# Node tiles 125 columns wide, laid side by side, in the mixer's operands and the turned layer norm of a graph layer on one Trainium2 core

## The chip, the cores and the metric

The kernel runs on one core of one Trainium2 chip. The metric is the device time of one execution in microseconds (us); lower is better. The time before is the median of three runs. The profile is of one further execution.

## The reference, cut to what matters

One GPS layer over a graph of 3125 nodes with 256 features: a normalised input, a graph convolution over 53125 edges, a linear-attention mixer over all nodes, and a mixture of 16 experts of which each node takes two.

```python
xn = layernorm(x)                                     # 3125 x 256
# graph convolution
agg = segment_sum(edge_weight[:, None] * xn[src], dst)
gnn = agg @ W.T + b
# linear attention, 8 heads of 32
Q, K = elu(xn @ Wq) + 1, elu(xn @ Wk) + 1
KV = sum over nodes of K (x) (xn @ Wv)                # per head
Z = 1 / (Q . sum(K) + eps)
msg = layernorm((Q KV Z) @ Wm) * g1 + b1
h = relu(concat([xn, msg]) @ W1) @ W2
mix = xn + layernorm(h) * g2 + b2
x = x + gnn + mix
# experts, on the normalised result
x = x + sum over the two best experts e of share_e * ((silu(y @ w1[e]) * (y @ w2[e])) @ w3[e])
```

## The kernel before

**Tiles.** The 3125 nodes are 25 tiles (`NT`) of 125 nodes (`V = 125`). A tile lies on the chip as 125 rows, one node to a partition, with three rows of padding up to `P = 128`. Where nodes run along columns (transposed operands), a tile has 128 columns, of which the last three belong to padding. All matrix products of 32-bit floats appear in the trace as two matmul records and two weight-load records each, products of 16-bit floats as one of each.

**Stage 1, node by node (to about 110 us).** For each tile, `normed` (line 409) makes the normalised rows `xn` and turns them with two transposes (line 428) into columns, which ScalarE copies into `xnT` (line 429), a buffer of 2 x 3200 columns. `projected` (line 431) uses the tile's 128 columns of `xnT` as the stationary operand (`lhsT`) against the weights `wcat` (lines 437 and 439), which gives the graph convolution's rows `y` (the product with W comes before the sum over edges), K and V; `y` stays in SBUF (`y_early`, `y_late`) and is also stored to `y_d` in DRAM by SyncE (line 449). `summed` (line 458) adds up K and V over the nodes; it already takes 125 rows. From tile 18 on, two adjacency blocks are built beside each tile.

**Adjacency (lines 328 to 360).** The edges become dense blocks: VectorE compares (`one`, line 335) and multiplies (`wone`, line 340), TensorE forms three products of 16-bit floats per block (line 355), ScalarE copies (line 358) and SyncE stores to `adj_d` in DRAM. All operands there have 128 columns.

**Stage 2, the mixer (about 110 to 550 us).** Seven groups of 4, 4, 4, 4, 3, 3 and 3 tiles. For a group of `nt` tiles the columns lie side by side, `w = nt * P` wide (512 or 384). `asked` (line 468) makes the queries: products with moving operand `xnT[..., c0 : c0 + w]` (line 477), the denominators with moving operand `qT` (line 489), a reciprocal and a product on VectorE in two parts (lines 494 and 495). `mixer` (line 631) takes for each tile a product with stationary `qT` (line 641), moments (`stats`, bn_stats and bn_aggr, lines 103 and 104), `rsqrt` (a chain of small VectorE instructions, lines 91 to 98), the norm (line 649), two transposes (line 653) and a copy into `mT` (line 654). This is the turned layer norm. Then the hidden layer with moving operands `xnT` and `mT`, `w` columns wide (line 662), its activation (line 664), and per tile a product with stationary `hT` (line 673). Pieces of `asked` for the next group, adjacency blocks and messages are traced between the pieces of the mixer. `messages` (line 613) multiplies dense adjacency rows, read back from `adj_d` as `nbr`, with `y` (line 625: stationary `rows`, 128 x 128; moving `y_of(k)`, 128 x 256), and adds the result to `x_all` on VectorE (line 627).

**Stage 3 (about 550 to 705 us).** `last_messages` (line 731) does the last part of the messages (line 738), beside the gate and the routing. **Stage 4** are the experts (lines 955 to 1077), which the change doesn't touch.

**What sets the order.** The build lays the instructions of each engine in an order of its own: what is ready sooner comes sooner, so the order in the trace isn't the order of the text (five transposes of line 309 stand between two halves of line 437's products). `tc.issue_after(ins)` puts what a block issues behind `ins` on its engine; it is used at the points where the order is fixed by hand. The rings of buffers set the rest: `tok` three PSUM buffers, `big` two, `pa` two, `pb` one, `nbr` three.

Of the kernel before, what the change touches and what calls it, by code (L numbers as in the profile page):

```python
# [8 lines left out]
F32 = mybir.dt.float32  # L9
# [53 lines left out]
def tile_gps_layer(ctx: ExitStack, tc: tile.TileContext, a: dict, out: bass.AP):  # L63
# [4 lines left out]
    dram = ctx.enter_context(tc.tile_pool(name="dram", bufs=1, space=DRAM))  # L68

    xn_d = dram.tile([N, XW], F32, name="xn_d")  # L70
    y_d = dram.tile([NT * P, C], F32, name="y_d")
    first_d = dram.tile([NG, 1], I32, name="first_d")


# [8 lines left out]

    def rsqrt(var, n, with_last=False):

        v = small.tile([P, 13], F32, name="rs_v")[:, :n]
        hv = small.tile([P, 13], F32, name="rs_h")[:, :n]
        bits = small.tile([P, 13], I32, name="rs_b")[:, :n]
        y = small.tile([P, 13], F32, name="rs_y")[:, :n]
        s = small.tile([P, 13], F32, name="rs_s")[:, :n]  # L90
        nc.vector.tensor_scalar(v, var, LN_EPS, None, op0=ALU.add)
        nc.vector.tensor_scalar(hv, v, -0.5, None, op0=ALU.mult)
        nc.vector.tensor_scalar(bits, v.bitcast(I32), 1, None, op0=ALU.logical_shift_right)
        nc.vector.tensor_scalar(y.bitcast(I32), bits, -1.0, float(0x5F3759DF), op0=ALU.mult, op1=ALU.add)
        for _ in range(3):
            nc.vector.tensor_tensor(s, y, y, op=ALU.mult)
            nc.vector.tensor_tensor(s, s, hv, op=ALU.mult)
            found = nc.vector.scalar_tensor_tensor(y, s, 1.5, y, op0=ALU.add, op1=ALU.mult)
        return (y, found) if with_last else y

    def stats(mv, src):
        st = small.tile([P, 6], F32, name="bn_st")
        nc.vector.bn_stats(st, src)
        return nc.vector.bn_aggr(mv, st)

# [88 lines left out]
    later.append((gate_w, a["gate_w"].rearrange("(k p) e -> p k e", p=128)))  # L194
    cb = w_mix.tile([P, C], F32, name="cb")

    xnT = w_mix.tile([128, 2, NT * P], F32, name="xnT")

    Y0 = PARTS[-1][0]
    y_early = w_mix.tile([P, Y0, C], F32, name="y_early")  # L200
# [2 lines left out]
    def y_of(t):  # L203
        return y_early[:, t, :] if t < Y0 else y_late[:, t - Y0, :]
# [204 lines left out]
    def normed(t):  # L409

        nonlocal rstd, r0
        for t0, t1 in BATCHES:
            if t == t0:
                rstd, r0 = ready.pop(t0), t0
        xn = work.tile([P, C], F32, name="xn", bufs=4)
        ins = nc.vector.tensor_scalar(xn, x_all[:, t, :], mv[:, t, 0:1], rstd[:, t - r0 : t - r0 + 1],
                                      op0=ALU.subtract, op1=ALU.mult)
        with tc.issue_after(ins.ins):
            for batch in BATCHES:
                if t == batch[0]:  # L420
                    factors(*batch, rstd)
            for _ in range(LISTS.get(t, 0)):
                next(pieces, None)
            if t in AHEAD:
                moments(*AHEAD[t])
        ptr = a_ps.tile([128, 2, P], F32, name="tok", bufs=3)
        for k in range(2):
            nc.tensor.transpose(ptr[:, k, :], xn[:, k * 128 : (k + 1) * 128], ident)
        nc.scalar.copy(xnT[:, :, t * P : (t + 1) * P], ptr)

    def projected(t):

        cols = slice(t * P, (t + 1) * P)
        pyk = a_ps.tile([P, 2 * C], F32, name="big")
        pv = a_ps.tile([P, C], F32, name="tok", bufs=3)
        for k in range(2):
            nc.tensor.matmul(pyk, lhsT=xnT[:, k, cols], rhs=wcat[:, k, : 2 * C], start=(k == 0), stop=(k == 1))  # L437
        for k in range(2):
            last = nc.tensor.matmul(pv, lhsT=xnT[:, k, cols], rhs=wcat[:, k, 2 * C :], start=(k == 0), stop=(k == 1))
        ek = work.tile([P, C], F32, name="ek", bufs=2)  # L440
        nc.scalar.activation(ek, pyk[:, C:], AF.Exp)
        k_sb = work.tile([P, C], F32, name="k_sb")
        nc.scalar.activation(k_sb, pyk[:, C:], AF.Relu)

        nc.vector.scalar_tensor_tensor(k_sb, ek, 1.0, k_sb, op0=ALU.min, op1=ALU.add)
        v_sb = v_ring[t % 3]
        v_copy = nc.scalar.activation(v_sb[:, :, :128], pv.rearrange("p (c v) -> p c v", c=2), AF.Copy, scale=1.0 / N)
        nc.scalar.copy(y_of(t), pyk[:, :C])
        stored = nc.sync.dma_start(y_d[t * P : (t + 1) * P, :], y_of(t))
        with tc.issue_after(stored.ins):  # L450
            load_later(t)

        with tc.issue_after(v_copy.ins):
            nc.scalar.activation(x_all[:, t, :], x_all[:, t, :], AF.Identity, scale=by[:, t : t + 1],
                                 bias=less[:, t : t + 1])
        return last, k_sb, v_sb
# [10 lines left out]

    def asked(t0, nt):

        w = nt * P  # L470
        c0 = t0 * P
        qT = mix.tile([128, 2, GROUP * P], F32, name="qT")
        asked_for.append(qT)
        for c in range(2):
# [12 lines left out]
        for c in range(2):  # L487
            p = a_ps.tile([128, 512], F32, name="big")
            nc.tensor.matmul(p[:, :w], lhsT=ksum[:, c, :], rhs=qT[:, c, :w], start=True, stop=True)  # L489
            pz.append((p, mix.tile([128, GROUP * P], F32, name="eq")))  # L490
        for part in (slice(0, 2 * P), slice(2 * P, w)):
            for c, (p, z) in enumerate(pz):
                nc.scalar.activation(z[:, part], p[:, part], AF.Copy, bias=ATT_EPS / N, scale=1.0 / N)
                nc.vector.reciprocal(z[:, part], z[:, part])
                nc.vector.tensor_tensor(qT[:, c, part], qT[:, c, part], z[:, part], op=ALU.mult)
            yield
# [62 lines left out]
    with tc.If(n_loops > 0):  # L559
        with tc.For_i(0, n_loops, 1) as it:  # L560
# [17 lines left out]
            nc.vector.tensor_scalar(took, took, -1.0, 1.0, op0=ALU.mult, op1=ALU.add)  # L578
            nc.vector.tensor_tensor(took, took, r.bitcast(F32)[:, 2:3], op=ALU.mult)
            t_d, _, p_d = placed(dst_f, sel, [V, 1], "ld")  # L580
            nc.vector.scalar_tensor_tensor(t_d, t_d, float(P), p_d, op0=ALU.mult, op1=ALU.add)
            row_d = sel.tile([V, 1], I32, name="l_row")
            nc.vector.tensor_copy(row_d, t_d)
            g = sel.tile([V, C], F32, name="l_g")
# [28 lines left out]
    def messages(part, t, n, alone=False):  # L613

        t0, t1 = PARTS[part]

        if alone:
            pb = bank_a(2 * C)[:P].rearrange("p (a b) c -> p a (b c)", a=2)
        else:
            pb = b_ps.tile([P, 2, C], F32, name="pb")  # L620
        for i in range(n):
            rows = neighbours(part, t + i)
            for k in range(t0, t1):

                nc.tensor.matmul(pb[:, i, :], lhsT=rows[:, k - t0, :], rhs=y_of(k),  # L625
                                 start=(k == t0 and i == 0), stop=(k == t1 - 1), skip_group_check=True)
        nc.vector.tensor_tensor(x_all[:, t : t + n, :], x_all[:, t : t + n, :], pb[:, :n, :], op=ALU.add)  # L627

    early = [(part, t, min(2, NT - t)) for part in range(len(PARTS) - 1) for t in range(0, NT, 2)]

    def mixer(t0, nt, qT, following):

        w = nt * P
        c0 = t0 * P
        mv = small.tile([P, GROUP, 2], F32, name="mv_m")
        mw = mix.tile([P, GROUP, C], F32, name="mw")
        for i in range(nt):
            cols = slice(i * P, (i + 1) * P)
            pw = a_ps.tile([P, C], F32, name="tok", bufs=3)
            for k in range(2):  # L640
                nc.tensor.matmul(pw, lhsT=qT[:, k, cols], rhs=kvw[:, k, :], start=(k == 0), stop=(k == 1))
            stats(mv[:, i, :], pw)
            nc.scalar.copy(mw[:, i, :], pw)
            yield
# [3 lines left out]
        for i in range(nt):  # L648
# [1 line left out]
                                    op0=ALU.subtract, op1=ALU.mult)  # L650
            ptr = a_ps.tile([128, 2, P], F32, name="tok", bufs=3)
            for k in range(2):
                nc.tensor.transpose(ptr[:, k, :], mw[:, i, k * 128 : (k + 1) * 128], ident)
            nc.scalar.copy(mT[:, :, i * P : (i + 1) * P], ptr)
            yield

        hT = mix.tile([128, 4, GROUP * P], F32, name="hT", bufs=1)
        for j in range(4):
# [6 lines left out]
            yield  # L665
            if next(following, "end") != "end":
                yield
        mv2 = small.tile([P, GROUP, 2], F32, name="mv_m2")
        hw = mix.tile([P, GROUP, C], F32, name="mw")
        for i in range(nt):  # L670
            po = a_ps.tile([P, C], F32, name="tok", bufs=3)
            for j in range(4):
                nc.tensor.matmul(po, lhsT=hT[:, j, i * P : (i + 1) * P], rhs=w2[:, j, :],  # L673
                                 start=(j == 0), stop=(j == 3))
            stats(mv2[:, i, :], po)
            nc.vector.scalar_tensor_tensor(hw[:, i, :], po, mv2[:, i, 0:1], g2, op0=ALU.subtract, op1=ALU.mult)
            if i < nt - 1:
                yield
        rstd = rsqrt(mv2[:, :nt, 1], nt)
        for i in range(nt):  # L680
            xt = x_all[:, t0 + i, :]
            nc.vector.scalar_tensor_tensor(xt, hw[:, i, :], rstd[:, i : i + 1], xt, op0=ALU.mult, op1=ALU.add)

    t = 0
# [38 lines left out]
    def bank_out():  # L723
        return bank("po", 3)
# [6 lines left out]
    def last_messages(t):  # L731
# [1 line left out]
        t0, t1 = PARTS[part]  # L733

        rows = neighbours(part, t, nbr_2 if t % 5 in (3, 4) else nbr)
        pg = bank_out()[:, 0, :]
        for k in range(t0, t1):
            last = nc.tensor.matmul(pg, lhsT=rows[:, k - t0, :], rhs=y_of(k), start=(k == t0),  # L738
                                    stop=(k == t1 - 1))
        nc.vector.tensor_tensor(x_all[:, t, :], x_all[:, t, :], pg, op=ALU.add)  # L740
        stats(mv_g[:, t, :], x_all[:, t, :])
        nc.sync.dma_start(out[t * V : (t + 1) * V, :], x_all[:V, t, :])
        return last
# [548 lines left out]
```

## Time and profile before

| | us |
|---|---|
| median of three runs (1036.63 to 1038.35) | 1038.11 |
| the profiled execution | 1038.03 |
| its span, from the first instruction to the last | 1036.2 |
| TensorE matmul busy, 6006 records | 1007.1 |
| TensorE weight loads busy, 6006 records | 809.3 |
| VectorE busy, 1750 instructions | 655.3 |
| ScalarE busy, 577 instructions | 263.9 |
| GpSimd busy, 200 instructions | 216.1 |

Busy time of an engine is the union of its instructions' times. Matmul records overlap: one of 256 columns is listed with some 382 ns, while the next begins some 216 ns behind it. So the step from one record to the next is read from runs of equal records (in the chain or the timeline), not from a record's own duration. A line such as L625 is a line of the kernel; in a group's line `out<-in` names the tiles, then come the shapes (rows x columns of the array, then partitions x elements), the count, the busy time, the mean of one in ns and the idle time before them.

### The profile page before, as it was taken

To read this page: it belongs to the slowest core of one execution; us is meant where nothing else is said; L and a number is where in the kernel's file an instruction comes from. 1 tells how busy PE (TensorE), PEld (TensorE's weight loads), DVE (VectorE), ACT (ScalarE), POOL (GpSimd) and SP (SyncE) were. 2 spreads that over 40 slices of the span, in tenths; PEclk is the share of its full clock that TensorE was granted. 3 is DMA by queue.
4 is the path that set the end of the run, shared out by engine and by line. 5 is a ranking of instruction groups with operands and counts; after the bars stand their busy time and mean duration, and the time that the engine had idled before them with its cause. 6 is when DMAs were issued, how large, how long until landed. Compare 5 with 4: busy or idle time off the path is not lost.

```text
span 1036.2 us, 16279 instructions
## 1 busy us (share of the span) xinstructions
PE 1007.1 (97%) x6006; PEld 809.3 (78%) x6006; DVE 655.3 (63%) x1750; ACT 263.9 (25%) x577; POOL 216.1 (21%) x200
## 2 busy tenths in 40 slices
PE   7999999999999999999999999999999999999995
PEld 5667666686786887887877888887888888888884
DVE  8968699889787897956598148786932222222221
ACT  3666424323323233222141000103111111111110
POOL 3420100023100000000000001014445444545442
PEclk9999999999999999999999999999999999999998
DMA  6444104343344344553354455565757757667662
GB/s 214 95 131 145 53 31 167 128 140 136 122 137 138 133 162 133 175 181 143 140 182 155 159 167 166 183 194 179 209 155 226 240 170 234 199 202 225 206 189 26
DMA packets 70374, 165.09 MB, mean 159 GB/s; under 512 B 11091, under 2 KB 29934, under 8 KB 66314
## 3 DMA queue, kind: packets, MB, share of 16 engines
q1 hardware_dynamic: 53816, 138.10, 38.9%
q0 software_dynamic: 15520, 25.04, 10.7%
q8 instruction: 50, 0.82, 0.3%
q10 hardware_dynamic: 946, 0.79, 0.2%
q14 instruction: 42, 0.34, 0.1%
HBM read 105.85 MB, written 58.00 MB: 158 GB/s over the span
## 4 chain that ended last, share of the span: by engine, by line
PE 71%; DVE 10%; issue 1%; POOL 0%; ACT 0%; POOLq 0%; DVEq 0%; ACTq 0%
PE ph L1001 18%; PE pb L625 13%; PE po L1027 10%; PE po L738 8%; PE pa L355 6%; PE big L662 6%; PE tok L673 3%; DVE wone L340 2%; PE ptr L987 1%; PE pa L625 1%; PE big L477 1%; DVE one L335 1%; PE ph L799 1%; DVE wone L350 1%; PE big L489 1%
## 5 line engine op out<-in xcount | busy, mean ns | idle before, releaser
L1001 PE MATMUL ph<-xTb,wt 128*128 128x256 f32 (+2 forms) x992 | 204.5, 355 | 0.8 <-issue 0.8
L1001 PEld LDWEIGHTS ph<-xTb,wt 128*128 128x128 f32 x992 | 171.5, 190 | 24.9 <-ACT xTb L990 4.5
L625 PE MATMUL pb<-y_early,nbr 128*128 128x256 f32 x736 | 170.7, 382 | 0.4 <-DVE x_all L627 0.4
L340 DVE TENSOR_TENSOR wone<-one,wgts 128x1536 bf16<-128x1536 bf16 x150 | 140.6, 949 | 27.0 <-PE pa L355 26.8
L625 PEld LDWEIGHTS pb<-y_early,nbr 128*128 128x128 f32 x736 | 135.4, 190 | 17.2 <-DVE x_all L627 1.0
L355 PEld LDWEIGHTS <-one 128*128 128x128 bf16 x1875 | 117.3, 97 | 39.1 <-issue 19.1
L358 ACT COPY adj<-pa 128x512 f32<-128x512 f32 (+1 forms) x157 | 91.8, 586 | 194.2 <-PE pa L355 156.4
L355 PE MATMUL pa<-wone,one 128*128 128x128 bf16 x1875 | 130.3, 218 | 2.3 <-DVE wone L340 0.9
L1008 DVE TENSOR_TENSOR hid<-hid,ph 128x512 f32<-128x512 f32 (+2 forms) x62 | 38.3, 618 | 145.7 <-PE ph L1001 135.4
L1027 PE MATMUL po<-wt,hid 128*128 128x256 f32 (+1 forms) x456 | 115.2, 385 | 0.8 <-DVE yb L1030 0.7
L738 PE MATMUL po<-y_late,nbr 128*128 128x256 f32 x450 | 102.3, 381 | 0.5 <-DVE x_all L627 0.5
L335 DVE TENSOR_TENSOR one<-iota,keys 128x1024 bf16<-128x1024 bf16 x150 | 100.8, 692 | 0.7 <-POOL wgts L317 0.7
L1031 POOL DMA_INDIRECT out<-yb,to_l x45 | 70.9, 1576 | 114.4 <-DVE yb L1030 63.4
L1027 PEld LDWEIGHTS po<-wt,hid 128*128 128x128 f32 (+1 forms) x456 | 79.1, 184 | 17.6 <-DVE yb L1030 5.5
L738 PEld LDWEIGHTS po<-y_late,nbr 128*128 128x128 f32 x450 | 83.4, 190 | 11.2 <-DVE x_all L627 0.9
L1007 ACT ACTIVATE hid<-ph 128x512 f32<-128x512 f32 (+2 forms) x62 | 33.6, 542 | 208.4 <-PE ph L1001 204.4
L1030 DVE TENSOR_SCALAR yb<-po,sh 128x256 f32<-128x256 f32 (+1 forms) x57 | 27.5, 482 | 57.3 <-PE po L1027 54.9
L751 POOL IOTA rev<- 125x16 f32 x1 | 0.2, 156 | 296.5 <-PE pb L625 296.5
L700 POOL TENSOR_TENSOR x_all<-x_all,cb 128x256 f32<-128x256 f32 x25 | 25.7, 1050 | 148.2 <-DVE x_all L627 140.5
L627 DVE TENSOR_TENSOR x_all<-x_all,pb 128x512 f32<-128x512 f32 (+1 forms) x37 | 24.3, 655 | 41.8 <-PE pb L625 41.8
L662 PE MATMUL big<-xnT,w 128*128 128x512 f32 (+1 forms) x112 | 49.8, 556 | 0.0
L437 PE MATMUL big<-wcat,xnT 128*128 128x512 f32 x100 | 49.0, 612 | 0.0
(285 smaller groups left out, 1202.5 us busy)
## 6 DMA issues: line engine op xcount, KB each, us to landing
wt<-in_w SPq DMA_DIRECT2D x28, 1536.0 KB
adj_d<-adj SPq DMA_DIRECT2D x156, 256.0 KB
nbr<-adj_d SPq DMA_DIRECT2D x25, 576.0 KB
nbr<-adj_d SPq DMA_DIRECT2D x50, 256.0 KB
nbr<-adj_d SPq DMA_DIRECT2D x25, 512.0 KB
wt<-in_w POOLq DMA_DIRECT2D x3, 1536.0 KB
out<-x_all SPq DMA_DIRECT2D x25, 125.0 KB
x_all<-in_x SPq DMA_DIRECT2D x4, 640.0 KB
```

The lines of the kernel that those rows point to most:

```text
L335: nc.vector.tensor_tensor(one.rearrange("p b h e j -> p (b h) e j"), iota_2[:, None, :, :].to_broadcast(shape), ql.rearrange("p b h j -> p ...
L340: nc.vector.tensor_tensor(wone, one[:, :, 1:2, :, :].to_broadcast(shape), w[:, :, :, None, :].to_broadcast(shape), op=ALU.mult)
L355: nc.tensor.matmul(pa[:, j, :], lhsT=one[:, j // 2, 0, :, j % 2], rhs=wone[:, j // 2, i, :, j % 2], start=(i == 0), stop=(i == 2))
L358: copied = nc.scalar.copy(rows[:, :n, :], pa[:, :n, :])
L437: nc.tensor.matmul(pyk, lhsT=xnT[:, k, cols], rhs=wcat[:, k, : 2 * C], start=(k == 0), stop=(k == 1))
L625: nc.tensor.matmul(pb[:, i, :], lhsT=rows[:, k - t0, :], rhs=y_of(k), start=(k == t0 and i == 0), stop=(k == t1 - 1), skip_group_check=True)
L662: nc.tensor.matmul(ph[:, :w], lhsT=w1[:, k, j * 128 : (j + 1) * 128], rhs=rhs, start=(k == 0), stop=(k == 3))
L738: last = nc.tensor.matmul(pg, lhsT=rows[:, k - t0, :], rhs=y_of(k), start=(k == t0), stop=(k == t1 - 1))
L1001: last = nc.tensor.matmul(p[:, m, :w], lhsT=self.wt[:, i, k * F + at : k * F + at + 128], rhs=self.xT[:, k, :w], start=(k == 0), stop=(k = ...
L1008: self.units = nc.vector.tensor_tensor(hid, hid, pre[1], op=ALU.mult)
L1027: last = nc.tensor.matmul(po[:n_r, r, :], lhsT=self.hid[:, k, r * LANES : r * LANES + n_r], rhs=self.wt[:, 2, k * C : (k + 1) * C], start= ...
L1031: made.append(nc.gpsimd.indirect_dma_start(out=out[:, :], out_offset=bass.IndirectOffsetOnAxis(ap=at, axis=0), in_=yb[:n_r, r, :], in_offs ...
```

## The change

Wherever nodes run along columns in the mixer's operands, a tile now takes 125 columns, not 128: in `xnT` (2 x 3125 columns), in `qT`, `mT` and `hT`, so that a group is 500 or 375 columns wide, not 512 or 384. The transposes that make these columns read 125 rows (lines 428 and 653). What has these columns as its stationary operand then has 125 rows of output, and moments, norms and copies on them take 125 partitions. The messages take 125 rows and 125 columns of the adjacency block and 125 rows of `y`; the adjacency itself is built, stored and loaded as blocks of 128 as before. `y_d` has 3125 rows, and its store takes 125 rows. No instruction is added or removed.

```diff
-    y_d = dram.tile([NT * P, C], F32, name="y_d")
+    y_d = dram.tile([N, C], F32, name="y_d")
...
     def rsqrt(var, n, with_last=False):
-        v = small.tile([P, 13], F32, name="rs_v")[:, :n]
+        p = var.shape[0]
+        v = small.tile([P, 13], F32, name="rs_v")[:p, :n]
...
-    xnT = w_mix.tile([128, 2, NT * P], F32, name="xnT")
+    xnT = w_mix.tile([128, 2, N], F32, name="xnT")
...
-            nc.tensor.transpose(ptr[:, k, :], xn[:, k * 128 : (k + 1) * 128], ident)
-        nc.scalar.copy(xnT[:, :, t * P : (t + 1) * P], ptr)
+            nc.tensor.transpose(ptr[:, k, :V], xn[:V, k * 128 : (k + 1) * 128], ident[:V, :V])
+        nc.scalar.copy(xnT[:, :, t * V : (t + 1) * V], ptr[:, :, :V])
...
     def projected(t):
-        cols = slice(t * P, (t + 1) * P)
-        pyk = a_ps.tile([P, 2 * C], F32, name="big")
+        cols = slice(t * V, (t + 1) * V)
+        pyk = a_ps.tile([P, 2 * C], F32, name="big")[:V]
...
-        stored = nc.sync.dma_start(y_d[t * P : (t + 1) * P, :], y_of(t))
+        stored = nc.sync.dma_start(y_d[t * V : (t + 1) * V, :], y_of(t)[:V])
...
     def asked(t0, nt):
-        w = nt * P
-        c0 = t0 * P
+        w = nt * V
+        c0 = t0 * V
...
-        for part in (slice(0, 2 * P), slice(2 * P, w)):
+        for part in (slice(0, 2 * V), slice(2 * V, w)):
...
-                nc.tensor.matmul(pb[:, i, :], lhsT=rows[:, k - t0, :], rhs=y_of(k),
+                nc.tensor.matmul(pb[:V, i, :], lhsT=rows[:V, k - t0, :V], rhs=y_of(k)[:V],
...
     def mixer(t0, nt, qT, following):
-        w = nt * P
-        c0 = t0 * P
-        mv = small.tile([P, GROUP, 2], F32, name="mv_m")
-        mw = mix.tile([P, GROUP, C], F32, name="mw")
+        w = nt * V
+        c0 = t0 * V
+        mv = small.tile([P, GROUP, 2], F32, name="mv_m")[:V]
+        mw = mix.tile([P, GROUP, C], F32, name="mw")[:V]
         for i in range(nt):
-            cols = slice(i * P, (i + 1) * P)
-            pw = a_ps.tile([P, C], F32, name="tok", bufs=3)
+            cols = slice(i * V, (i + 1) * V)
+            pw = a_ps.tile([P, C], F32, name="tok", bufs=3)[:V]
...
-                nc.tensor.transpose(ptr[:, k, :], mw[:, i, k * 128 : (k + 1) * 128], ident)
-            nc.scalar.copy(mT[:, :, i * P : (i + 1) * P], ptr)
+                nc.tensor.transpose(ptr[:, k, :V], mw[:, i, k * 128 : (k + 1) * 128], ident[:V, :V])
+            nc.scalar.copy(mT[:, :, i * V : (i + 1) * V], ptr[:, :, :V])
...
-                nc.tensor.matmul(po, lhsT=hT[:, j, i * P : (i + 1) * P], rhs=w2[:, j, :],
+                nc.tensor.matmul(po, lhsT=hT[:, j, i * V : (i + 1) * V], rhs=w2[:, j, :],
...
     def last_messages(t):
-        pg = bank_out()[:, 0, :]
+        pg = bank_out()[:V, 0, :]
...
-            last = nc.tensor.matmul(pg, lhsT=rows[:, k - t0, :], rhs=y_of(k), start=(k == t0),
+            last = nc.tensor.matmul(pg, lhsT=rows[:V, k - t0, :V], rhs=y_of(k)[:V], start=(k == t0),
```

The same cut (`[:V]`) is made on the rows of `ek`, `k_sb`, `v_sb`, `y_of(t)`, `x_all`, `pv`, `po`, `hw` and `g2` where these lines use them.

## The prediction

> **What bounds the kernel now.** I read the busy shares first, then the chain that ended last, then the waits, then the groups by shape and single stretches of the timeline. The page's shares, and its chain by engine:
>
> ```profile
> PE 1007.1 (97%) x6006; PEld 809.3 (78%) x6006; DVE 655.3 (63%) x1750; ACT 263.9 (25%) x577; POOL 216.1 (21%) x200
> ...
> PE 71%; DVE 10%; issue 1%; POOL 0%; ACT 0%; POOLq 0%; DVEq 0%; ACTq 0%
> ```
>
> TensorE (PE) works for 97% of the span, and 71% of the chain is PE (this view loses the chain before 171 us, so its shares add up to 82%). A busy share alone proves little for PE, since its records overlap. So the waits of PE between 100 and 560 us, where the mixer runs:
>
> ```profile
> PE tok L653 <- DVE mw L649: 4.2, 5, 1.3
> PE tok L641 <- DVEq L559: 1.0, 1, 1.0
> PE big L489 <- ACT eq L493: 0.8, 1, 0.8
> ...
> PE pa L355 <- DVE wone L340: 0.4, 1, 0.4
> ```
>
> Columns: total us, times, longest. With four further waits of 0.4 to 0.6 us they make 8.3 us in 460. The one that repeats is the turned norm: PE's transposes (L653) wait for VectorE's norm (L649). Everywhere else PE's own rate is the time, so what counts is how long each matmul record holds PE. Three pieces of the chain give that, as start, length, what:
>
> ```profile
> 198.87 3.43 PE big L662 x8
> ...
> 400.53 2.63 PE big L662 x8
> ...
> 432.17 6.96 PE pb L625 x32
> ```
>
> Eight records of 512 moving columns took 3.43 us, 429 ns each; eight of 384 columns 2.63 us, 329 ns each; 32 of 256 columns 6.96 us, 217.5 ns each. (429 - 217.5) / 256 = 0.83 ns for each moving column of a 32-bit record, with only some 5 ns besides. The weight load (190 ns listed, overlapped) doesn't show in it.
>
> **What the change saves on PE.** Only moving operands along which nodes run get shorter; these are the groups:
>
> ```profile
> L662 PE MATMUL big<-xnT,w 128*128 128x512 f32 x64 | 31.2, 599 | 0.0
> L662 PE MATMUL big<-mT,w 128*128 128x512 f32 x64 | 30.5, 597 | 0.5 <-ACT mT L654 0.5
> ...
> L662 PE MATMUL big<-xnT,w 128*128 128x384 f32 x48 | 18.6, 500 | 0.0
> ```
>
> L662: 128 records go from 512 to 500 columns and 96 (48 from xnT, 48 from mT) from 384 to 375: 128 x 12 + 96 x 9 = 2400 columns. L477 (the groups list 32 and 24 records): 600. L489 (16 and 12): 300. The transposes L428 and L653, 50 records each, go from 128 to 125 columns: 300. Together 3600 columns x 0.83 ns = **3.0 us**. Line 437, 439, 641, 673, 625 and 738 have 125 stationary columns instead, and still 256 or 512 moving ones; at 0.83 ns per moving column they hold PE as long as before. I take 0 for them.
>
> That zero is the largest claim here, since these lines are 100 + 100 + 100 + 200 + 800 + 450 = 1750 records that get a stationary operand of 125 columns; the 1250 of L625 and L738 among them, and the 100 transposes, get 125 rows as well. The timeline of before has such shapes already (start, length, what):
>
> ```profile
> 61.30 0.61 PE L461 MATMUL pkv<-v_sb,k_sb 125*128 125x129 f32 x4
> 61.75 0.70 PE L309 MATMUL pa<-ident,key 125*128 125x125 f32 x5
> 62.28 0.38 PE L428 MATMUL tok<-ident,xn 128*128 128x128 f32 x2
> ```
>
> L461 takes 125 rows: the next record begins 0.45 us (61.75 - 61.30) after four of them, 113 ns each; L309, 125 rows and 125 moving columns, 0.53 us for five, 106 ns each; L428, 128 rows and columns, 110 ns each (62.28 to 62.50 for two). So 125 rows cost nothing over 128. Half of L461's moving operands start at byte 516 of their buffer (the second half of 2 x 129 columns), and the four still take 0.45 us: a start off a round boundary, as `xnT[..., t * 125]` now has, costs nothing either. For 125 stationary columns the weight loads say:
>
> ```profile
> L625 PEld LDWEIGHTS pb<-y_early,nbr 128*128 128x128 f32 x736 | 135.4, 190 | 17.2 <-DVE x_all L627 1.0
> L355 PEld LDWEIGHTS <-one 128*128 128x128 bf16 x1875 | 117.3, 97 | 39.1 <-issue 19.1 <-DVE wone L340 5.8 <-DVE wone L350 1.5
> ...
> L852 PEld LDWEIGHTS <-ones_h 125*125 125x125 bf16 x3 | 0.4, 138 | 0.2
> ...
> L243 PEld LDWEIGHTS pa<-heads,ones 125*125 125x125 f32 x2 | 0.3, 189 | 0.0
> ```
>
> A 16-bit load takes 97 ns with 128 columns and 138 ns with 125: 41 ns dearer for less work. A 32-bit load takes 190 ns with 128 and 189 ns with 125 (two records only). All loads that this change narrows are of 32-bit floats; the 16-bit ones (the adjacency, L355) keep 128. The Trainium skill, "TensorE: Matmul & The Clock Gate", section "Weight-path perf modes — Fast Weight Load (FWL) and DoubleRow", says that the fast load is on when the number of weights is 128 and the type isn't FP32; by that rule no narrowed load here was ever fast, and the sum is unchanged; the pair 97 / 138 agrees with it, and 190 / 189 too. Bounds for these 1750 loads: none below -3 ns each (three columns of a load; L1027's 64-column loads list 136 ns against 190, so 0.84 ns a column), hidden under 216 ns of matmul; above, 41 ns each, which is a rival below.
>
> **What else moves.** VectorE: the reciprocals L494 take 1726 ns for 256 columns and 936 for 128, 6.2 ns a column; 150 columns fewer over the seven groups, 0.9 us; L495 and L483 some 0.4 us. ScalarE: the copies and activations on these columns (L429, L654, L480, L481, L493, L664) lose 1050 columns at 0.85 ns, 0.9 us. These lie beside PE, so I count them at nothing; where they stand right before a wait of PE (L493 before L489, one wait of 0.8 us) they help by some 10 ns. Instructions on 125 instead of 128 partitions with the same number of elements per partition cost the same (L627, L649, L676 and the moments). SyncE: the stores to y_d (L449) take 125 rows; their issue lists 320 ns with 128 rows, and the stores of 125 rows to `out` (L742) list 289, and nobody waits for either. The loads of `nbr` and the stores of `adj_d` stay at 128. No wait is added and no step is moved in the text.
>
> **How much of the 3.0 us arrives at the end.** Before 171 us, PE runs nearly back to back. Behind it the chain holds 5.6% x 1036.2 = 58 us of L662, where 184 of its 224 records stand (40 come earlier), 184 / 224 of 128 x 429 + 96 x 329 ns = 71 us: four fifths are on the path. The rest lies under stretches in which the chain runs over VectorE, the norms of each group and the last adjacency blocks (514 to 563 us). A fifth of what L662, L477 and L489 save behind 171 us (2.7 us in all, less 0.7 before) is 0.4; the first transposes before 15 us, which wait for loads, and a few of L653 are 0.1. The norms' chain itself starts from a product on PE (L641), so it starts earlier with PE, and the gain in front of it is kept. **3.0 - 0.5 = 2.5 us.** The profiled execution took 1038.03 (span 1036.2, 1.8 around it): 1035.5; the median lies 0.08 above it, so 1035.6 against 1038.11, 0.24% less. About 0.2% (2.1 us) is what a measurement of this kernel can tell from no change, so this forecast stands just outside it.
>
> **The rivals.** (a) *VectorE swallows it.* From 200 to 400 us VectorE is busy 170 of 200 us; where its adjacency work ends last, PE would only wait longer. Kept would be what falls into 30 to 171 us (some 0.8 us: 40 records of L662, 20 of L477, 8 of L489 at 10 ns, and transposes) and into 400 to 514 us (some 0.6): 1.4 us less, 1036.7, within 0.2%. Against it: PE waits only 0.4 us for `wone` L340 in the whole stretch.
> (b) *The order turns against PE* (the other side). The build orders by readiness: L309 sits between the halves of L437 above. With shorter records it can set one more adjacency block on VectorE (L335 and L340, 692 + 949 = 1641 ns) ahead of a norm (L649), and PE waits at L653, as it does 4.2 us in all now. One block in each of the seven groups would be 11.5 us, 9.0 net: 1047.1. It decides from three groups on: 4.9 - 2.5 = +2.4 us, 1040.5; four give 1042.2. With one or two it ends within 0.2%. It could as well take some of the 4.2 us away: 4.1 of it gives 1031.5.
> (c) *Neighbours at 500 bytes are taken for overlapping*, so that each projection (L437) waits for the copy of the next tile's columns (L429, 365 ns, 0.3 us behind the transposes): 0.6 us x 24 = 14 us, 1050. Against it: ScalarE's L454 reads single 4-byte columns of `by` beside others that are written, and shows no wait for them.
> (d) *Narrow 32-bit loads are dearer like the 16-bit ones*: 190 + 41 = 231 ns against a step of 216; if a load, listed at its full length, then set the step, 15 ns x 1650 records with 256 moving columns = 25 us, 1060. Against it: the 100 records of L799, with 16 moving columns and full loads, keep PE busy for 13.3 us in all, so loads follow each other within 133 ns, and 133 + 41 would still hide under 216.
> (e) *Part of the array is dear*: four transposes of a short block, two with 64 rows (788.67 us), take 0.94 us, four full ones (798.49) 0.60, so 0.17 us for each short one. At 125 rows that would add over 200 us; L461 and L309 exclude it.
>
> **How the numbers follow.** Forecast, 2.1 to 3.2 us gained: 0.53. (a): 0.18, within. (b): 0.25, of it 0.13 slower, 0.05 within, 0.07 faster than forecast. (c) 0.03 and (d) with (e) 0.01, slower. Faster 0.60, same 0.23, slower 0.17. The range reaches from (b)'s lucky end, 1031.5, to its four groups, 1042.2; it leaves out (c), (d), (e) and the worst of (b), some 0.13. The forecast's own range is 1034.9 to 1036.0.
>
> **What would show it.** After: eight records of L662 in 3.35 us (500 columns) and 2.5 or so (375); L625 and L738 still 216 ns apart; 125-column 32-bit loads near 188 ns; L437 with no wait for L429. Wrong if L653's waits rise beyond 4.2 us by as much as PE saves, if L625's step moves by even 2 ns (1250 records, 2.5 us), or if the instructions' order differs in the mixer.

## The result and the profile after

| | before | changed |
|---|---|---|
| median of 17 runs each, us | 1037.6 | 1034.88 |
| ratio, with its 95% interval | | 0.9977 (0.9971 to 0.9984) |
| span of the profiled execution, us | 1036.2 | 1033.0 |
| from the first matmul of L641 to the last of L738, us | 121.8 to 706.8 | 120.8 to 703.7 |

The changed kernel is 0.23% faster, 2.4 us, with an interval from 1.7 to 3.0. (The ratio compares the means of the runs, 1035.3 and 1037.6; the medians lie 2.7 us apart.) In the new file all lines from 86 on have moved by one, so L626 there is L625 before. The page, busy shares and chain by engine:

```profile
PE 1004.1 (97%) x6006; PEld 804.3 (78%) x6006; DVE 654.8 (63%) x1750; ACT 263.1 (25%) x577; POOL 215.7 (21%) x200
...
PE 70%; DVE 11%; issue 2%; ACT 0%; POOL 0%; POOLq 0%; ACTq 0%; DVEq 0%
```

TensorE is as full as before and 3.0 us less busy, with the same 6006 records (2.2 us less, 1004.9, in r1, a second profile of the changed kernel). The waits of PE from 100 to 560 us:

```profile
PE tok L654 <- DVE mw L650: 4.4, 5, 1.4
PE tok L642 <- DVEq L560: 0.9, 1, 0.9
PE big L490 <- ACT eq L494: 0.8, 1, 0.8
...
PE pa L356 <- DVE wone L341: 0.4, 1, 0.4
```

They hardly changed: the norm costs 4.4 us instead of 4.2, `wone` 0.4 as before. So most of what PE saved didn't turn into waits. Pieces of the chain (start, length, what):

```profile
197.30 3.35 PE big L663 x8
...
397.94 2.58 PE big L663 x8
...
429.44 6.96 PE pb L626 x32
```

Eight records of 500 columns take 3.35 us instead of 3.43, ten ns less each, and eight of 375 take 2.58. The messages, now with 125 rows and 125 stationary columns, take 6.96 us for 32 as before, to the hundredth. In stage 1 (start, length, what):

```profile
60.59 0.61 PE L462 MATMUL pkv<-v_sb,k_sb 125*128 125x129 f32 x4
61.04 0.70 PE L310 MATMUL pa<-ident,key 125*128 125x125 f32 x5
61.57 0.38 PE L429 MATMUL tok<-ident,xn 125*128 125x125 f32 x2
61.78 1.02 PE L438 MATMUL big<-wcat,xnT 128*125 128x512 f32 x2
```

The two turned blocks of L429 take 0.21 us to the next record, not 0.22, and the projection L438 follows at once: it waits for no neighbour's copy, and no such wait stands in the whole list of PE's waits. The weight loads (busy us, mean ns):

```profile
L626 PEld LDWEIGHTS pb<-y_early,nbr 125*125 125x125 f32 x736 | 133.7, 188 | 18.6 <-DVE x_all L628 1.0
L356 PEld LDWEIGHTS <-one 128*128 128x128 bf16 x1875 | 117.3, 97 | 39.1 <-issue 18.8 <-DVE wone L341 6.3 <-DVE wone L351 2.3
```

A narrow 32-bit load is 2 ns shorter, 188 for 190.

Lined up record by record, PE in the changed kernel is 0.7 us ahead at 52 us and 3.1 us ahead at 578 us, and the lead stays near that. The growth between is 2.4 us. The 0.7 is chance of the first stretch: r1 is 0.4 us behind at 52 us and 2.0 us ahead at 578, again 2.4 us of growth; and e1, which has the instructions of before there, is 0.3 us ahead at 52. A single profile moves by this much elsewhere too: e1 falls back by 1.5 us near 180 us, at a wait for a load of `nbr`, and r1 gains 1.0 us near 700 us, where a wait of 0.7 us isn't there. In some of these profiles, of either kernel, the granted clock is half for a few us in the first 30 (mean 0.94 there before and in r1, 1.00 in the first profile of the changed kernel).

The growth can be set beside the prediction's sum, stretch by stretch (us): what the columns saved in a stretch come to at 0.83 ns each, and by how much the lead grows there.

| stretch, us | sum | changed | r1 |
|---|---|---|---|
| 52 to 120 | 0.26 | 0.26 | 0.27 |
| 120 to 171 | 0.52 | 0.37 | 0.35 |
| 171 to 500 | 1.90 | 1.72 | 1.72 |
| 500 to 578 | 0.25 | 0.09 | 0.07 |
| together | 2.9 | 2.4 | 2.4 |

Split by line, from the start of a record to the start of the next with listed waits taken off, the five shortened lines (L663, L478, L490, L429, L654) hold PE 2.3 us less in both profiles; all other lines together change by less than 0.1 us, and the listed waits by -0.2. Behind 500 us, where little arrives, three steps from L663 to L356 take 363, 565 and 641 ns, where others take 315: PE waits there for VectorE's last `wone` (L351).

### The profile page after: what moved, and what is told of

The parts are those of the page before. It is cut to its first block, busy times and chain, and to the rows that moved or that the text cites. A ratio compares the mean times of both kernels' runs of the same rounds, so it can differ in the third digit from the quotient of the medians.

```text
span 1033.0 us, 16284 instructions
## 1 busy us (share of the span) xinstructions
PE 1004.1 (97%) x6006; PEld 804.3 (78%) x6006; DVE 654.8 (63%) x1750; ACT 263.1 (25%) x577; POOL 215.7 (21%) x200
## 3 DMA queue, kind: packets, MB, share of 16 engines
q1 hardware_dynamic: 53466, 138.02, 39.3%
## 4 chain that ended last, share of the span: by engine, by line
PE 70%; DVE 11%; issue 2%; ACT 0%; POOL 0%; POOLq 0%; ACTq 0%; DVEq 0%
PE ph L1002 17%; PE pb L626 13%; PE po L1028 10%; PE po L739 8%; PE pa L356 6%; PE big L663 5%; PE tok L674 3%; DVE wone L341 2%; PE pa L626 1%; PE ptr L988 1%; PE big L478 1%; DVE one L336 1%; DVE wone L351 1%; PE ph L800 1%; PE big L490 1%
## 5 line engine op out<-in xcount | busy, mean ns | idle before, releaser
L626 PE MATMUL pb<-y_early,nbr 125*125 125x256 f32 x736 | 170.6, 382 | 0.4 <-DVE x_all L628 0.4
L626 PEld LDWEIGHTS pb<-y_early,nbr 125*125 125x125 f32 x736 | 133.7, 188 | 18.6 <-DVE x_all L628 1.0
L356 PEld LDWEIGHTS <-one 128*128 128x128 bf16 x1875 | 117.3, 97 | 39.1 <-issue 18.8
L359 ACT COPY adj<-pa 128x512 f32<-128x512 f32 (+1 forms) x157 | 91.8, 586 | 195.5 <-PE pa L356 169.4
L356 PE MATMUL pa<-wone,one 128*128 128x128 bf16 x1875 | 130.5, 219 | 2.1 <-DVE wone L341 0.9
L739 PE MATMUL po<-y_late,nbr 125*125 125x256 f32 x450 | 102.3, 381 | 0.5 <-DVE x_all L628 0.5
L739 PEld LDWEIGHTS po<-y_late,nbr 125*125 125x125 f32 x450 | 82.4, 188 | 12.1 <-DVE x_all L628 0.9
L628 DVE TENSOR_TENSOR x_all<-x_all,pb 125x512 f32<-125x512 f32 (+1 forms) x37 | 24.3, 658 | 41.7 <-PE pb L626 41.7
L663 PE MATMUL big<-xnT,w 128*128 128x500 f32 (+1 forms) x112 | 48.8, 548 | 0.0
L674 PE MATMUL tok<-w,hT 128*125 128x256 f32 x200 | 47.9, 383 | 0.0
```

The source lines that it names most:

```text
L356: nc.tensor.matmul(pa[:, j, :], lhsT=one[:, j // 2, 0, :, j % 2], rhs=wone[:, j // 2, i, :, j % 2], start=(i == 0), stop=(i == 2))
L359: copied = nc.scalar.copy(rows[:, :n, :], pa[:, :n, :])
L626: nc.tensor.matmul(pb[:V, i, :], lhsT=rows[:V, k - t0, :V], rhs=y_of(k)[:V], start=(k == t0 and i == 0), stop=(k == t1 - 1), skip_group_ch ...
L663: nc.tensor.matmul(ph[:, :w], lhsT=w1[:, k, j * 128 : (j + 1) * 128], rhs=rhs, start=(k == 0), stop=(k == 3))
L674: nc.tensor.matmul(po, lhsT=hT[:, j, i * V : (i + 1) * V], rhs=w2[:, j, :], start=(j == 0), stop=(j == 3))
L739: last = nc.tensor.matmul(pg, lhsT=rows[:V, k - t0, :V], rhs=y_of(k)[:V], start=(k == t0), stop=(k == t1 - 1))
```

## The experiments

All ratios are to the kernel before on the same chip, with 95% intervals.

| run | median us | before us | ratio |
|---|---|---|---|
| e1 messages alone at 125 | 1038.5 | 1038.5 | 1.000 (0.9991 to 1.0009) |
| e2 changed, adjacency's stationary columns and its transfers at 125 | 1140.92 | 1038.5 | 1.099 (1.0975 to 1.1005) |
| e3 changed, adjacency's moving columns at 125 | 1038.28 | 1038.5 | 1.000 (0.9991 to 1.0009) |
| e4 changed, a fifth of L663's columns left out | 1186.33 | 1038.5 | 1.142 (1.1404 to 1.1439) |
| e5 as e3, columns spaced by 128 | 1033.14 | 1036.29 | 0.9971 (0.9961 to 0.9981) |
| e6 changed, stationary columns at 125 in two of three products | 1036.12 | 1036.29 | 1.000 (0.9991 to 1.0009) |
| e7 changed, loads of nbr at 125 rows | 1069.74 | 1036.29 | 1.0328 (1.0312 to 1.0344) |
| e8 changed, messages' stationary columns back at 128 | 1034.06 | 1036.29 | 0.9981 (0.9972 to 0.999) |
| r1 changed, again | 1035.0 | 1036.97 | 0.9982 (0.9973 to 0.9991) |
| r2 as e5, again | 1034.36 | 1036.97 | 0.9977 (0.9968 to 0.9986) |

**e1 and e8: where the gain isn't.** Edit of e1, in the kernel before; e8 undoes the column part in the changed kernel:

```diff
-                nc.tensor.matmul(pb[:, i, :], lhsT=rows[:, k - t0, :], rhs=y_of(k),
+                nc.tensor.matmul(pb[:V, i, :], lhsT=rows[:V, k - t0, :V], rhs=y_of(k)[:V],
```

> The kernel before with the messages alone narrowed (lines 625 and 738: 125 rows, 125 stationary columns; everything else at 128). Theory (the step between two matmul records is set by their moving columns, 0.83 ns each): the 1250 records keep their step of 216 ns, so the time is that of before within 0.1% (0 us, at most 1 us either way). Rival (shorter weight loads count): 1250 loads of 188 in place of 190 ns, each 2 to 2.5 ns less, would give 2.5 to 3.1 us less and so explain the whole gain; rival (narrow 32-bit loads are dearer): up to 18 us more.

> The changed kernel with the messages' stationary operand back at 128 columns (lines 626 and 739; still 125 rows). The other half of e1: all that is gained should be there still, ratio to before 0.9977 (0.997 to 0.9985), 1250 records at 216 ns. Rival (the shorter loads of the messages carry the gain): ratio 1.000.

Measured: e1 has the time of before, e8 that of the changed kernel. The 1250 narrowed records of the messages give nothing and cost nothing (to within the 0.9 us of e1's interval), and their step is 216 ns in both. The rival in which 2 ns of each load count falls.

**e4: a larger dose of the same saving.**

```diff
+        cut = w * 4 // 5
+        nc.gpsimd.memset(hT[:, :, cut:w], 0.0)
...
-                rhs = xnT[:, k, c0 : c0 + w] if k < 2 else mT[:, k - 2, :w]
+                rhs = xnT[:, k, c0 : c0 + cut] if k < 2 else mT[:, k - 2, :cut]
```

> The changed kernel with a fifth of the columns of the mixer's hidden layer left out (line 663 takes 400 or 300 moving columns, not 500 or 375; GpSimd sets the rest of hT to zero). A larger dose of the same saving: 128 x 100 + 96 x 75 = 20000 columns x 0.83 ns = 16.6 us of PE. Theory (PE's columns are the time here): some four fifths arrive, 13 us less than the changed kernel, 1022. Rival (VectorE, busy 85% in 200 to 400 us, takes over soon): the larger part turns into waits of PE for wone and for the norm, and under 8 us arrive, 1027 or more.

The whole time says nothing here: with other numbers out of the mixer the gate sends other nodes to other experts, and the kernel then runs more expert steps (6694 PE records, not 6006). I had not thought of that. Up to the end of the messages the work is the same but for these columns (3743 PE records in either kernel), so the stretch from the first record of `kvw` to the last of `y_late` can be compared (count, duration min/median/max, first and last start). Changed kernel:

```profile
L642 PE MATMUL tok<-kvw,qT x100: 377/379/481, 120.8 to 516.5; 128*125 128x256 f32 x100
...
L739 PE MATMUL po<-y_late,nbr x450: 377/379/481, 587.9 to 703.7; 125*125 125x256 f32 x150
```

The kernel of e4:

```profile
L642 PE MATMUL tok<-kvw,qT x100: 377/379/481, 123.2 to 505.4; 128*125 128x256 f32 x100
...
L741 PE MATMUL po<-y_late,nbr x450: 377/379/482, 574.8 to 690.7; 125*125 125x256 f32 x150
```

703.7 - 120.8 = 582.9 against 690.7 - 123.2 = 567.5: 15.4 us less, of the 16.7 by which L663's own steps got shorter. So 92% arrives, even of a dose over five times that of the change. VectorE doesn't take over; that rival falls.

**e2, e6 and e7: what a narrow adjacency would cost.** Edits of e2 (e6 has the first alone, for the second and third product; e7 the last alone):

```diff
-                nc.tensor.matmul(pa[:, j, :], lhsT=one[:, j // 2, 0, :, j % 2], ...
+                nc.tensor.matmul(pa[:V, j, :], lhsT=one[:, j // 2, 0, :V, j % 2], ...
...
-        nc.sync.dma_start(to(adj_d[part]), rows[:, :n, :])
+        nc.sync.dma_start(to(adj_d[part]), rows[:V, :n, :])
...
-        nc.sync.dma_start(rows, flat.rearrange("(p t l) -> p t l", p=P, l=P))
+        nc.sync.dma_start(rows[:V], flat.rearrange("(p t l) -> p t l", p=V, l=P))
```

> The changed kernel, and besides the adjacency's stationary operand of 16-bit floats at 125 columns (its moving one stays at 128; its copies, stores and the loads of nbr take 125 rows). The load should go from 97 to 137 ns as listed. If the step between the matmuls hides it, it stays at 57 to 60 ns (two records of 125 columns at before's line 852 began 56 and 68 ns apart from the next): 0 to +5.6 us over the changed kernel (1034.9), so 1035 to 1040.5. Rival: the load's 41 ns come on top of each of the 1875 records: +77 us, 1112, or about half of it if it is overlapped in part.

e2 lost 104 us against the changed kernel (spans 1136.9 and 1033.0), and neither theory had the cause. Its PE waits:

```profile
PE pb L626 <- DMA nbr<-adj_d: 30.6, 12, 6.5
PE pa L356 <- ACT adj L359: 19.6, 7, 8.0
PE po L739 <- DMA nbr<-adj_d: 15.2, 10, 3.6
PE pa L626 <- DMA nbr<-adj_d: 10.2, 2, 7.4
```

Loads that landed before PE asked for them now end its longest waits, though they carry 2.3% fewer bytes. The second line is the stores: ScalarE's copy of a block (L359) now waits for an earlier block's store, and PE for the copy. ScalarE's waits for it (total us, times, longest) in the changed kernel, and then in e2:

```profile
ACT adj L359 <- DMA adj_d<-adj: 2.4, 3, 1.1
```

```profile
ACT adj L359 <- DMA adj_d<-adj: 163.0, 69, 10.0
```

The page's SyncE queue (packets, MB, share of 16 engines) in the changed kernel, and then in e2:

```profile
q1 hardware_dynamic: 53466, 138.02, 39.3%
```

```profile
q1 hardware_dynamic: 49814, 136.09, 33.0%
```

Counting how many packets of this queue are under way at each moment from 200 to 500 us, the changed kernel has 16 or 17 for 77 us and 5 or 6 for 8 us; e2 has 5 or 6 for 287 of the 300 us. So a transfer of 128 rows has sixteen packets under way at once, one of 125 rows five, which I read as sixteen and five DMA engines. The packet counts agree: before to changed, 53816 to 53466 is 350 = 25 stores of `y_d` x (3 rows + 11 four-byte packets), eleven engines fewer that report the end. The Trainium skill, "DMA: Bandwidth & Descriptors", section "Why a DMA increments its semaphore by 16 and not by 1", says that a transfer uses the largest number of engines up to 16 that divides the size of the slowest dimension on both sides. For 125 that is five, and the counts here agree with it.

> The changed kernel with 125 stationary columns in the second and third of the adjacency's three products (1250 of 1875 records, 16-bit); every copy, store and load stays at 128 rows. It takes e2's two suspects apart. Theory (e2's 103 us come from its transfers of 125 rows, which run five at a time and not sixteen): only PE's step counts, 57 to 60 ns on 1250 records: +3.8 us over the changed kernel, ratio to before 1.000 to 1.002. Rival (the slower 16-bit weight load, 139 against 97 ns, makes the loss): two thirds of e2's loss, +70 us, ratio 1.065.

> The changed kernel with the loads of nbr at 125 rows and nothing else; the order of the instructions is that of the changed kernel. Theory (a transfer of 125 rows has five packets in flight, one of 128 has sixteen): 2.3% fewer bytes, but each load takes about three times as long; PE waits at L626 for it. More than half of e2's loss, +50 to +100 us, ratio 1.05 to 1.10. Rival (the stores of 125 rows in e2 made the loss, the loads are hidden by three buffers): within 5 us of the changed kernel.

The changed kernel itself wasn't run on the chip of e5 to e8; e8, which has its time, stands for it. e6 is 2.1 us above e8, so the narrow 16-bit load makes 2 us and not 70. The load itself did slow down (e6, both widths in one kernel, line 357 there):

```profile
L357 PEld LDWEIGHTS <-one 128*125 128x125 bf16 x1250 | 114.4, 138 | 21.5 <-issue 14.2
...
L357 PEld LDWEIGHTS <-one 128*128 128x128 bf16 x625 | 61.0, 98 | 16.7 <-DVE wone L341 5.4 <-issue 3.7 <-DVE wone L351 2.1
```

138 against 98 ns. But only some 3 ns of the 40 show in the step from record to record (median 60 for 57): loads that are listed with 138 ns follow each other every 60 ns, so they overlap. The rule of the Trainium skill that the prediction cited ("TensorE: Matmul & The Clock Gate", section "Weight-path perf modes — Fast Weight Load (FWL) and DoubleRow") agrees with the two loads; what losing the fast load costs in time is the measured 2 us.

e7 stands 35.7 us above e8, with the instructions in the same order: the transfers are the cause, as expected, but loads alone make a third of e2's loss, less than the half I had expected. Its PE waits begin with:

```profile
PE po L739 <- DMA nbr<-adj_d: 18.5, 13, 3.8
PE pa L626 <- DMA nbr<-adj_d: 7.8, 1, 7.8
```

With three buffers the slower loads are hidden in the mixer (1.7 us lost by 570 us). The loss comes from a single wait of 7.8 us behind 570 us and from the last part of the messages. There PE takes the rows of a tile, nine blocks, every 4 to 7 us in the changed kernel, and the loads don't keep up (last record of L739 at 739.0 us, not 703.7). Part of it isn't waiting. In e7 the granted clock is half for 17 us between 580 and 711 us, where the changed kernel has the full clock throughout, and records of L739 then step by 427 ns, not 216. PE is busy for 13 us of these 17, so by estimate some 7 of the 36 us are lost to the clock; in e2 it is half for 65 us between 180 and 800 us, PE busy for 49 of them, some 24 of the 104. The rest of e2's loss beyond loads alone and the narrow 16-bit load, some 66 us with its share of the clock, is left to the narrow stores, whose waits the lines of L359 show, or to both on one queue; stores alone were not tried.

**e3 and e5: the adjacency's moving side.**

```diff
-        wone = hot.tile([128, 2, 3, P, 2], BF16, name="wone")
+        wone = hot.tile([128, 2, 3, V, 2], BF16, name="wone")                    # e3
+        wone = hot.tile([128, 2, 3, P, 2], BF16, name="wone")[:, :, :, :V]       # e5
...
-                nc.tensor.matmul(pa[:, j, :], lhsT=one[...], rhs=wone[...]
+                nc.tensor.matmul(pa[:, j, :V], lhsT=one[...], rhs=wone[...]
```

> The changed kernel, and besides the adjacency's moving operand at 125 columns (its stationary one stays at 128; adj_d, adj and nbr get 125 columns to a block). If PE's moving columns set the time: 1875 records x 3 x 0.42 ns (16-bit, half the 0.83 of a 32-bit record) = 2.3 us less than the changed kernel; with VectorE's wone (36 of 1536 columns, 22 ns x 150 = 3.3 us) on the path in its stretches some 0.5 us more: 1032.1 to 1032.9. Rival: a 16-bit record of 128 moving columns is held by its weight load (97 ns listed, step 57 ns) and not by its columns: then 0 from PE, and 0 to 0.8 us from VectorE.

> The kernel of e3 (adjacency with 125 moving columns), but wone's columns lie 128 apart again, so that each moving operand starts at a multiple of 512 bytes as in the changed kernel, not of 500. In e3 the step of these 1875 records rose from 57 to 60 ns though they have three columns fewer. If the start of the operand does that: steps of 56 ns, 1875 x 1.25 ns = 2.3 us less than the changed kernel, ratio to before about 0.9955. Rival (125 moving columns of 16 bits are dear by themselves): 60 ns again and a ratio of 1.000 as e3.

e3 came out slower than the changed kernel: with three columns fewer the mean step between its 16-bit records, within runs of them, is 60.0 ns instead of 57.6. e5 has the same columns and the same transfers with starts at multiples of 512 bytes, and 57.6. So operands that start at multiples of 500 bytes cost 2.4 ns a record here on average, 1875 x 2.4 = 4.5 us of PE, of which some 3 show in the ratios of e3 and e5 (1.000 and 0.9971). But three columns fewer save nothing, where 1.25 ns were expected: these records aren't held by their columns. That half of e3's rival holds; that the weight load is what holds them isn't shown. Not every start costs the same: within e3's runs the records that start at 0 or 2000 bytes of `wone` step by 57 to 60 ns, those at 500, 1000, 1500 and 2500 bytes by 59 to 62. No run says which property of the start decides. What e5 gains over e8 on its chip, 0.9 us, would then be VectorE's 21 ns less per `wone` (932 for 953).

> The changed kernel itself, beside r2 on one chip, to settle which of the two is the better: ratio to before 0.9977, as measured first.

> The kernel of e5 (16-bit moving operand of the adjacency at 125 columns, spaced by 128) beside the changed kernel. If VectorE's shorter wone (1500 for 1536 elements, 150 instructions) is worth what e5 showed, it ends 0.9 us below r1, ratio to before 0.9965 to 0.9972; if e5 was chance, the two agree within 0.3 us.

r2 ended 0.6 us below r1, with intervals that overlap widely. Both beat the kernel before; that e5's version beats the changed kernel isn't settled.

## Why the prediction was right

Forecast 1035.6, 0.24% less; measured 0.23% less. That the two agree so closely is luck, since the interval reaches from 0.16% to 0.29%. In microseconds the median, 1034.88, lies 0.7 below the forecast, because the kernel before ran at 1037.6 in its 17 runs and not at the 1038.11 of the first three.

- **The price of a column** held: 0.83 ns, read from pieces of 256 and 512 columns, gives 10 ns for 12 columns, and 10 ns were measured (429 to 419 by record starts); nine columns gave 7.5 to 8 ns (median 323 to 315). PE's summed busy time fell by the 3.0 us of the sum in one profile and by 2.2 in the other, so it is too rough to confirm the sum; the split by line is better, with 2.3 us on the shortened lines and next to nothing on all others.
- **Zero for the 1750 records with narrow stationary operands** held: 216 ns before and after, and e1 and e8 each show it in the time. The rows that carried it (L461, L309, L243) had few records, but the right shapes. That an odd start of the moving operand costs nothing, read from L461, is a little off: L663's records that read `xnT` from byte 9500 step by 318 ns, others of 375 columns by 314 or 315. Too few records have it to matter.
- **How much arrives** held as well: 0.5 of 3.0 us was taken off, and in the stretches of the table 2.4 of 2.9 arrive. The reason, VectorE in the last adjacency blocks, shows behind 500 us (0.09 of 0.25). But nearly as much is lost between 120 and 171 us (0.37 of 0.52), where the prediction took PE to run nearly back to back, so the size is in part luck. And e4, with its larger dose on L663 alone, lost 8%, not 20%.
- **The rivals.** (a) VectorE swallows it: only in the last adjacency blocks, where 0.2 us are lost; from 171 to 500 us nine tenths arrive, and e4 shows the same at five times the dose. (b) The order turns: it did, in a small part. 24 of 6006 PE records changed places, all between 542 and 562 us, in the last adjacency blocks. The prediction named a changed order in the mixer as a sign of being wrong; here it cost nothing that can be seen, since the lead is 3.1 us ahead of that stretch and behind it, and L654's waits rose by 0.2 us. An order held fixed wasn't tried. (c) No projection waits for its neighbour. (d) Narrow 32-bit loads are cheaper, 188 ns. (e) The step of 125-row records is that of 128.
- **What the prediction passed over:** that a store of 125 rows runs five packets at a time and not sixteen. It said of `y_d` only that nobody waits, which is why the outcome held: the changed kernel does narrow that store, and no instruction waits for it. The same edit on `nbr` costs 36 us in e7.

## What to carry to other kernels

A matmul record of 32-bit floats that PE runs back to back costs here what its moving columns cost (the 16-bit records of 128 columns didn't), so padding along nodes is paid for only where nodes lie on the moving side; count those columns and leave the rest at zero. Before narrowing a tile to a number of rows that sixteen doesn't divide, look for the transfers that use it: here 125 rows in place of 128 turned hidden loads into a loss of 36 us. And a part that is left out to raise a dose must not feed a decision later in the kernel, or only the time up to there can be read.

## What the runs showed of the hardware that was not expected

- A transfer of 125 rows has five packets under way at a time, one of 128 sixteen (5 or 6 at most moments of e2 against 16 or 17 in the changed kernel's transfers).
- 16-bit moving operands that start at multiples of 500 bytes take 60.0 ns a record, at multiples of 512 bytes 57.6. On the 32-bit records of L663, whose `xnT` operands start at multiples of 500 bytes as well, most starts cost nothing (315 ns for 375 columns, 419 for 500); a few cost 2 to 4 ns (318 ns at byte 9500).
- Three moving columns fewer save nothing on a 16-bit record of 128 (57.6 ns either way), and 2.5 ns or so on a 32-bit one.
